# Ten query blocks' score maxima crossed over the partitions by VectorE and a line in DRAM, in an attention and mixture-of-experts kernel

## The chip, the core and the metric

The kernel runs on one core of one Trainium2 chip. The time is device microseconds of one launch; the profile is one further execution, taken by the hardware profiler. Engines are named as in the profile: PE (TensorE, with PEld for its weight loads), DVE (VectorE), ACT (ScalarE), POOL (GpSimd) and SP (SyncE), whose queue of DMA issues is shown as SPq.

## What is computed

One layer in float32, on 4096 tokens of 256 features: causal attention with one head of 256, then eight experts of which each token takes two.

```python
# x: (1, 4096, 256)
z = layernorm(x)
Q, K, V = z @ Qw, z @ Kw, z @ Vw
scores = Q @ K.T / sqrt(256) + causal_mask
x = x + softmax(scores) @ V

h = layernorm(x) @ W_in + b_in
probs = softmax(h @ W_gate + b_gate)            # 8 experts
topv, topi = top_k(probs, 2); topv /= topv.sum()
mid = relu(h @ W1[e] + b1[e])                   # for the experts taken
x = x + (sum_e topv[e] * (mid @ W2[e] + b2[e])) @ W_out + b_out
```

The softmax subtracts, from each query's scores, the largest of them. That maximum is what this change is about.

## The kernel before

**Layout.** Scores are held transposed: keys on the 128 partitions, queries along the free dimension. A query block is 256 queries (`QB`); there are sixteen, numbered 0 to 15. A chunk is 256 keys (two key tiles of 128). Block n needs chunks 0 to n. `scores(n)` makes, for each chunk, eight PE instructions into one PSUM tile `ps` (four such tiles exist, shared under the tag "mm" with the tiles `pq` and `ph`), a copy to SBUF by ACT (`s`, L564), and a running maximum over chunks by DVE (`mx`, L570). At its end DVE folds the two halves of `mx` and the diagonal chunk into `top`, 128 partitions by 256 queries (L588 to L591): on each partition, for each query, the largest of the scores that this partition holds. What is still wanted is the maximum over the partitions, and that on every partition.

**The maximum over the partitions before.** It is done in the inner function `finish` of `scores`. PE turns `top` in two 128 by 128 squares into PSUM (`pt`, L598), DVE reduces along the free dimension (`m`, L603), and PE turns `m`, broadcast, back in two more squares (`pmax`, L608). Then DVE subtracts `pmax` from every chunk of the block's scores (L612, and L618 for the diagonal chunk) and ACT takes the exponentials (L615, L621).

**The loop.** Iteration g computes `scores(g + 1)`, then `attend(g)`: for each chunk c of block g eight PE instructions (six for the diagonal one) accumulate `po` (two tiles under the tag "o", of which there are two in all, shared with the tiles `pv` of `values` and `pk` of `route`). After chunk c `attend` runs what stands in the list `between[c]`; from iteration 4 on (`CALM`) that is where `finish` of block g + 1 is put, at chunk min(g - 2, 4), with its first turn kept in program order on PE. At the end of `attend` DVE takes the reciprocal of the sums (`rinv`, L645) and adds the result to `x` (L647), which sets `po` free.

Around that, in even iterations `project` (`pq` on PE, copied to `qT` by DVE at L518) and `values` (`pv`, L526) follow for the next 512 tokens, and from iteration 6 on `send` runs at chunk 5: `ph` on PE (L362, four tiles that take all four "mm" tiles), then `lg` and `hr` on DVE (L372, L373), then two DMAs of `hr` to DRAM (`rows`, L375). In iterations 3 and 5 `send` comes ahead of `attend`. `route` (L399 to L458, with the matmuls `pk` at L423 and L428) follows the iteration of its `send`, or in iterations 3 and 5 its `attend`.

**SP's queue.** Each 512 tokens' normalised rows are turned, twice per 512 tokens (`zT` for the attention, `z1T` for the experts), by a DVE transpose of 32 by 32 squares (L329) and sixteen DMAs from SP (`move` in `turn_todo`, L334), each of 32 KB. So nearly every iteration of the attention has one set of sixteen DMAs in SP's queue. SP issues in order, and an issue that waits holds what is behind it.

**Order.** The framework's scheduler lists the instructions of each engine in an order of its own, by priority (program order) among what it takes to be ready; `tc.keep_in_program_order` pins an instruction. The order on each engine is fixed before the run.

Of the kernel before, what the change touches and what calls it, by code (L numbers as in the profile page):

```python
# [10 lines left out]
F32 = mybir.dt.float32  # L11
I32 = mybir.dt.int32
AF = mybir.ActivationFunctionType
ALU = mybir.AluOpType
AX = mybir.AxisListType
SP = mybir.EngineType.SP

P = 128
# [3 lines left out]
QB = 256  # L22
# [6 lines left out]
SQ = 32  # L29
LATE = 2  # L30
USUAL = 6
CALM = 4
# [5 lines left out]
def preln_attention_moe_kernel(  # L38
# [18 lines left out]
    nc = tc.nc  # L57
# [3 lines left out]
    NT = S // P  # L61
# [28 lines left out]
    dram = ctx.enter_context(tc.tile_pool(name="dram", bufs=1, space=bass.MemoryType.DRAM))  # L90
    attn = ctx.enter_context(tc.tile_pool(name="attn", bufs=1))
# [14 lines left out]
    slots = dram.tile([NE * R, LINE], I32, name="slots")  # L106
    bias1 = dram.tile([NE * P, NF], F32, name="bias1")
    parts = dram.tile([TOPK * S, D], F32, name="parts")


    zeros = const.tile([P, P], F32, tag="zeros", name="zeros")
# [46 lines left out]
    for b in range(1, NB):  # L158
# [13 lines left out]
        out=mask,  # L172
        in_=mask,
        compare_op=ALU.is_ge,
        fill=MASKED,
# [360 lines left out]
    KU = QB // P  # L536
    QPB = TB // QB

    def scores(g, fill=()):

        b, q = divmod(g, QPB)
        parts_of = min(max(g - 1, 1), 4)
        ss, mx = [], None
        top = attn.tile([P, QB], F32, tag="top", name=f"top{g}", bufs=2)
        for c in range(g + 1):
            ps = ps_mm(f"ps{g}_{c}")
            s = piece(f"s{g}_{c}", KU, QB)
            ss.append(s)  # L550
            for u in range(KU):
                kt = c * KU + u
                lo = u * P if c == g else 0
                for d in range(ND):
                    nc.tensor.matmul(  # L555
                        ps[:, u * QB + lo : (u + 1) * QB],
                        lhsT=zT[kt // TPB][:, kt % TPB, d, :],
                        rhs=qT[b][:, d, q * QB + lo : (q + 1) * QB],
                        start=(d == 0),
                        stop=(d == ND - 1),  # L560
                    )
            flat = s.rearrange("p u q -> p (u q)")
            if c < g:
                nc.scalar.copy(flat, ps)  # L564
                if c == 0:
                    mx = flat
                else:
                    old = mx
                    mx = attn.tile([P, TB], F32, tag="mx", name=f"mx{g}_{c}", bufs=2)
                    done = nc.vector.tensor_tensor(mx, ps, old, ALU.max)  # L570
                    for do in fill[len(fill) * (c - 1) // parts_of : len(fill) * c // parts_of]:
                        if done:
                            tc.keep_in_program_order(done)
                        done = do()
                    if fill and done:
                        tc.keep_in_program_order(done)
                continue
            for u in range(KU):
                on = slice(u * P, (u + 1) * P)
                nc.vector.tensor_tensor(  # L580
                    s[:, u, on], ps[:, u * QB + u * P : u * QB + (u + 1) * P], mask, ALU.add
                )
                if u + 1 < KU:
                    nc.scalar.copy(s[:, u, (u + 1) * P :], ps[:, u * QB + (u + 1) * P : (u + 1) * QB])
            if mx is None:
                nc.vector.tensor_copy(top, s[:, 0, :])
            else:
                nc.vector.tensor_tensor(top, mx[:, :QB], mx[:, QB:], ALU.max)  # L588
                nc.vector.tensor_tensor(top, top, s[:, 0, :], ALU.max)
            for u in range(1, KU):  # L590
                nc.vector.tensor_tensor(  # L591
                    top[:, u * P :], top[:, u * P :], s[:, u, u * P :], ALU.max
                )
        def finish(behind=False):

            pt = ps_tr(f"pt{g}")
            for u in range(KU):
                done = nc.tensor.transpose(pt[:, ts(u, P)], top[:, ts(u, P)], ident)  # L598
                if behind:
                    tc.keep_in_program_order(done)  # L600
                    behind = False
            m = attn.tile([P, KU], F32, tag="m", name=f"m{g}", bufs=2)
            nc.vector.tensor_reduce(  # L603
                m, pt[:, :QB].rearrange("p (u k) -> p u k", k=P), AX.X, ALU.max
            )
            pm = ps_tr(f"pmax{g}")
            for u in range(KU):
                nc.tensor.transpose(pm[:, ts(u, P)], m[:, u : u + 1].to_broadcast([P, P]), ident)  # L608
            for c in range(g + 1):
                s = ss[c]  # L610
                if c < g:
                    nc.vector.tensor_tensor(  # L612
                        s, s, pm[:, :QB].unsqueeze(1).to_broadcast([P, KU, QB]), ALU.subtract
                    )
                    nc.scalar.activation(s, s, AF.Exp)  # L615
                    continue
                for u in range(KU):
                    nc.vector.tensor_tensor(  # L618
                        s[:, u, u * P :], s[:, u, u * P :], pm[:, u * P : QB], ALU.subtract
                    )  # L620
                    nc.scalar.activation(s[:, u, u * P :], s[:, u, u * P :], AF.Exp)  # L621

        return ss, finish

# [413 lines left out]
    for e in range(NE):  # L1038
# [23 lines left out]
        out=slots.rearrange("(p n r) o -> p n (r o)", p=P, r=SB // LINE),  # L1062
        in_=empty.unsqueeze(1).to_broadcast([P, NE * R // P * LINE // SB, SB]),
# [5 lines left out]
        out=rows[TOPK * (S - LATE * TB) :, :].rearrange("(t p) d -> p t d", p=P),  # L1069
        in_=zero.unsqueeze(1).to_broadcast([P, TOPK * (LATE * TPB + 1), D]),  # L1070
    )

    row, finish = scores(0)
# [4 lines left out]
    fill, lg, got, hTs = [], None, {}, {}  # L1078
    for g in range(NT // KU):
        b, q = divmod(g, QPB)  # L1080

        between = {}
        nxt = None
        if g + 1 < NT // KU:

            nxt, finish = scores(g + 1, fill)
            if g < CALM:
                finish()
            else:
                between[min(g - 2, 4)] = [partial(finish, True)]  # L1090
        fill = []
        if q == 0 and b == NB - 1:

# [4 lines left out]
        if q == 0 and b > 0:  # L1098

            def send(behind=False, b=b):  # L1100
                nonlocal lg
                lg = enter(b - 1, z1T, attn, behind)

            if b - 1 >= EASY[1]:
                between[5] = [partial(send, True)]
        if q == 0 and b == NB - 1:

            def fetch_first():
                for n in range(AHEAD):
                    got[n] += fetch_weights(work[n])  # L1110

            def find():
                nonlocal seen
                seen = route(b - 1, lg, seen, attn, True)

            between[6], between[11] = [fetch_first], [find]
            weighed = AHEAD
        elif g == 0:
            turn(0, 1, ahead, zT[1])
# [210 lines left out]
```

## Time and profile before

| | |
|---|---|
| median of 3 runs | 1080.48 us (1079.9 to 1081.41) |
| profiled execution | 1071.75 us, span 1070.0 us |
| granted TensorE clock | 1.0 |
| busy in the span: PE, PEld | 1062.3 us, 882.9 us |
| DVE, ACT, POOL | 674.6 us, 332.4 us, 236.9 us |
| turns `pt` (L598) | 32 instructions, 7.1 us |
| turns `pmax` (L608) | 32 instructions, 6.1 us |
| reduction `m` (L603) | 16 instructions, 423 ns each |
| SP's DMAs for `zT` and `z1T` | 96 and 112 issues of 32 KB |

Busy time of a group counts stretches of time, so that overlapped instructions are not counted twice; the mean of one instruction is its own length. The timeline gives the start in microseconds from the start of the span, the time covered, engine, line, operation, what is written and read, and how many were merged into the line; in square brackets stands the engine's idle time before it and what ended that. The attention lies between about 20 and 565 us; iterations 4 to 13, which the change touches, between about 83 and 479 us.

### The profile page before, as it was taken

How to read it: one execution, taken by the hardware profiler on the slowest of the kernel's cores; microseconds unless marked ns; L12 is line 12 of the kernel's file. 1: busy time of each engine (PE TensorE's matmuls, PEld its weight loads, DVE VectorE, ACT ScalarE, POOL GpSimd, SP SyncE). 2: the span in 40 equal slices, each digit the busy share in tenths (PEclk: the TensorE clock that was granted, in tenths of full speed). 3: DMA queues.
4: the chain of work that ended last, by engine and by line, in shares of the span. 5: the costliest groups of instructions: out<-in, count | busy, mean ns of one | idle time of the engine just before them, and what ended most of it. 6: DMA issues, size and time to landing. Idle time of an engine off the chain costs nothing.

```text
span 1070.0 us, 15770 instructions
## 1 busy us (share of the span) xinstructions
PE 1062.3 (99%) x4973; PEld 882.9 (83%) x4973; DVE 674.6 (63%) x2114; ACT 332.4 (31%) x730; POOL 236.9 (22%) x289
## 2 busy tenths in 40 slices
PE   9999999999999999999999999999999999999998
PEld 6788888888888888888888887777778787777887
DVE  5877667564655546254665724858588786767636
ACT  2232233322432323242402221232323332323254
POOL 2104043103103000201222522232322322313110
PEclk9999999999999999999999999999999999999999
DMA  9422211121011011001655475887889896969285
GB/s 313 104 54 44 58 25 51 17 54 24 6 45 25 8 21 39 3 1 21 202 170 180 124 248 180 280 266 268 279 269 315 262 333 213 335 211 327 77 300 187
DMA packets 177995, 158.80 MB, mean 148 GB/s; under 512 B 82158, under 2 KB 157875, under 8 KB 177909
## 3 DMA queue, kind: packets, MB, share of 16 engines
q1 hardware_dynamic: 168980, 139.67, 42.4%
q0 software_dynamic: 8384, 17.58, 5.1%
q8 instruction: 40, 0.66, 0.3%
q10 hardware_dynamic: 544, 0.52, 0.1%
q14 instruction: 47, 0.38, 0.1%
HBM read 124.79 MB, written 26.38 MB: 141 GB/s over the span
## 4 chain that ended last, share of the span: by engine, by line
PE 97%; DVE 2%; POOL 0%; DMA 0%; issue 0%; SPq 0%; ACT 0%; DVEq 0%; POOLq 0%
PE po L633 21%; PE ps L555 21%; PE pm_a L921 11%; PE pe_a L988 11%; PE pe_b L988 5%; PE pm_b L921 5%; PE ph L362 3%; PE pm_c L951 3%; PE pf L1209 3%; PE pe_c L988 3%; PE pq L511 3%; PE pv L526 2%; PE pe_d L988 2%; PE pm_d L951 2%; PE pm_z L921 1%; PE pe_z L988 1%
## 5 line engine op out<-in xcount | busy, mean ns | idle before, releaser
L633 PE MATMUL po<-v,s 128*128 128x257 f32 x1056 | 237.9, 380 | 0.0
L555 PE MATMUL ps<-qT,zT 128*128 128x256 f32 x1088 | 233.3, 374 | 0.0
L555 PEld LDWEIGHTS ps<-qT,zT 128*128 128x128 f32 x1088 | 203.1, 190 | 28.0 <-issue 1.0
L633 PEld LDWEIGHTS po<-v,s 128*128 128x128 f32 x1056 | 197.2, 190 | 26.7
L564 ACT COPY s<-ps 128x512 f32<-128x512 f32 x120 | 70.2, 585 | 171.9 <-PE ps L555 132.6
L988 PE MATMUL pe_a<-w_a,mid_a 128*128 128x256 f32 x544 | 121.6, 380 | 0.0
L921 PE MATMUL pm_a<-hT_a,w_a 128*128 128x256 f32 x544 | 120.0, 379 | 0.0
L988 PEld LDWEIGHTS pe_a<-w_a,mid_a 128*128 128x128 f32 x544 | 102.6, 190 | 19.0 <-issue 5.6
L570 DVE TENSOR_TENSOR mx<-ps,mx 128x512 f32<-128x512 f32 x91 | 62.9, 691 | 83.7 <-ACT s L564 82.9
L930 ACT ACTIVATE mid_a<-pm_a,c_a 128x256 f32<-128x256 f32 x136 | 64.2, 472 | 165.1 <-PE pm_a L921 150.4
L921 PEld LDWEIGHTS pm_a<-hT_a,w_a 128*128 128x128 f32 x544 | 103.4, 190 | 14.1
L615 ACT ACTIVATE s<-s 128x512 f32<-128x512 f32 x120 | 72.2, 630 | 100.2 <-DVE s L612 100.2
L901 DVE STREAM_TRANSPOSE hT_a<-h_a 32x128 f32<-32x128 f32 x272 | 82.2, 302 | 3.8
L443 POOL DMA_INDIRECT slots<-assign,ati x64 | 62.5, 977 | 77.5 <-DVE ati L441 58.7
L612 DVE TENSOR_TENSOR s<-s,pmax 128x512 f32<-128x512 f32 x120 | 73.0, 679 | 7.3 <-PE pmax L608 7.3
L997 POOL DMA_INDIRECT parts<-y_a,slot_a x34 | 34.2, 1005 | 167.4 <-DVE y_a L996 138.0
L893 DVE STREAM_TRANSPOSE mid_c<-raw_c 32x256 f32<-32x256 f32 x128 | 55.8, 436 | 1.9
L988 PE MATMUL pe_b<-w_b,mid_b 128*128 128x256 f32 x256 | 56.8, 380 | 0.0
L921 PE MATMUL pm_b<-hT_b,w_b 128*128 128x256 f32 x256 | 56.6, 379 | 0.0
L988 PEld LDWEIGHTS pe_b<-w_b,mid_b 128*128 128x128 f32 x256 | 48.5, 190 | 9.4 <-issue 2.8
L921 PEld LDWEIGHTS pm_b<-hT_b,w_b 128*128 128x128 f32 x256 | 48.6, 190 | 6.6
L930 ACT ACTIVATE mid_b<-pm_b,c_b 128x256 f32<-128x256 f32 x64 | 30.1, 470 | 63.0 <-PE pm_b L921 63.0
(280 smaller groups left out, 1163.5 us busy)
## 6 DMA issues: line engine op xcount, KB each, us to landing
w_a<-in_L_ffn_W_dram SPq DMA_DIRECT2D x68, 512.0 KB, 6.0
w_d<-in_L_ffn_W_dram SPq DMA_DIRECT2D x48, 512.0 KB, 6.8
w_c<-in_L_ffn_W_dram SPq DMA_DIRECT2D x32, 512.0 KB, 8.1
w_b<-in_L_ffn_W_dram SPq DMA_DIRECT2D x32, 512.0 KB, 7.8
rows<-hr SPq DMA_DIRECT2D x16, 512.0 KB, 3.2
yp<-parts SPq DMA_DIRECT2D x14, 512.0 KB, 7.0
x<-in_L_attn_x_dram SPq DMA_DIRECT2D x7, 512.0 KB, 4.2
z1T<-z SPq DMA_DIRECT2D x112, 32.0 KB, 2.0
```

The lines of the kernel that those rows point to most:

```text
L443: put = nc.gpsimd.indirect_dma_start(out=slots, out_offset=bass.IndirectOffsetOnAxis(ap=ati[:, j : j + 1], axis=0), in_=assign[:, TOPK * ( ...
L555: nc.tensor.matmul(ps[:, u * QB + lo : (u + 1) * QB], lhsT=zT[kt // TPB][:, kt % TPB, d, :], rhs=qT[b][:, d, q * QB + lo : (q + 1) * QB], ...
L564: nc.scalar.copy(flat, ps)
L570: done = nc.vector.tensor_tensor(mx, ps, old, ALU.max)
L612: nc.vector.tensor_tensor(s, s, pm[:, :QB].unsqueeze(1).to_broadcast([P, KU, QB]), ALU.subtract)
L615: nc.scalar.activation(s, s, AF.Exp)
L633: nc.tensor.matmul(po[u][:, : D + 1], lhsT=ss[c][:, k, ts(u, P)], rhs=vb[kt // TPB][:, kt % TPB, :], start=(kt == 0), stop=(kt == g * KU + u),
L893: pin(do())
L901: pin(do())
L921: nc.tensor.matmul(pm[:, :SB], lhsT=w1[c][:, ts(f, P)], rhs=hT[:, c, :], start=(c == 0), stop=(c == ND - 1),)
L930: nc.scalar.activation(mid[f // 2][:, f % 2, :], pm[:, :SB], AF.Relu, bias=c1[:, f : f + 1])
L988: nc.tensor.matmul(pe[ts(j, rest), :D], lhsT=mid[f][:, ts(u, P)][:, ts(j, rest)], rhs=w2[f // (NF // 2)][:, f % (NF // 2), :], start=(f == 0),
```

## The change

For the blocks 5 to 14, whose scores are made in iterations 4 to 13 (`far`), the maximum over the partitions no longer goes through PE. At the end of `scores` the new function `spread_top` transposes `top` in place in 32 by 32 squares on DVE, reduces each square's rows (`m4`, 128 by 8), copies the four groups of 32 partitions beside each other (`c4`) and reduces over them (`m`, 32 by 8). SP writes `m` to a line of 256 numbers in DRAM (`tops`, two lines used in turn), and reads that line back, broadcast to 128 partitions, into `top`. `finish` then subtracts `top` from SBUF in place of `pmax` from PSUM. It is put two chunks later: after chunk min(g - 1, 6). The six other blocks keep the turns, now in the function `top_by_pe`.

```diff
+    tops = dram.tile([2, QB], F32, name="tops")
...
-    def scores(g, fill=()):
+    def scores(g, fill=(), far=False):
...
+        def spread_top():
+            nc.vector.transpose(top, top)
+            m4 = attn.tile([P, QB // SQ], F32, tag="m4", name=f"m4_{g}", bufs=2)
+            nc.vector.tensor_reduce(
+                m4, top.rearrange("p (b k) -> p b k", k=SQ), AX.X, ALU.max
+            )
+            c4 = attn.tile([SQ, P // SQ, QB // SQ], F32, tag="c4", name=f"c4_{g}", bufs=2)
+            for k in range(P // SQ):
+                nc.vector.tensor_copy(c4[:, k, :], m4[ts(k, SQ), :])
+            m = attn.tile([SQ, QB // SQ], F32, tag="m1", name=f"m1_{g}", bufs=2)
+            nc.vector.tensor_reduce(m, c4.rearrange("p k b -> p b k"), AX.X, ALU.max)
+            home = tops[g % 2 : g % 2 + 1, :]
+            nc.sync.dma_start(out=home.rearrange("o (b i) -> (o i) b", i=SQ), in_=m)
+            nc.sync.dma_start(out=top, in_=home.to_broadcast([P, QB]))
+
+        if far:
+            spread_top()
+
         def finish(behind=False):
-            pt = ps_tr(f"pt{g}")
-            ...
-            for u in range(KU):
-                nc.tensor.transpose(pm[:, ts(u, P)], m[:, u : u + 1].to_broadcast([P, P]), ident)
+            pm = top if far else top_by_pe(behind)
             for c in range(g + 1):
...
+        def top_by_pe(behind):
+            # the turns and the reduction as they stood in finish
+            ...
+            return pm
...
-            nxt, finish = scores(g + 1, fill)
+            far = CALM <= g < NT // KU - 2
+            nxt, finish = scores(g + 1, fill, far)
             if g < CALM:
                 finish()
             else:
-                between[min(g - 2, 4)] = [partial(finish, True)]
+                between[min(g - 1, 6) if far else 4] = [partial(finish, True)]
...
-                between[5] = [partial(send, True)]
+                between.setdefault(5, []).append(partial(send, True))
...
-            between[6], between[11] = [fetch_first], [find]
+            for c, do in ((6, fetch_first), (11, find)):
+                between.setdefault(c, []).append(do)
```

## The prediction

> **What bounds the kernel now.** I read the page's busy line and its chain first, then the chain in order of time through iterations 4 to 13, then the timeline of SP's queue, then all engines together where a wait could reach PE.
>
> ```profile
> PE 1062.3 (99%) x4973; PEld 882.9 (83%) x4973; DVE 674.6 (63%) x2114; ACT 332.4 (31%) x730; POOL 236.9 (22%) x289
> PE 97%; DVE 2%; POOL 0%; DMA 0%; issue 0%; SPq 0%; ACT 0%; DVEq 0%; POOLq 0%
> ```
>
> PE is busy for 99% of the span and is 97% of the chain that ended last, at a granted clock of 1.0. What leaves PE leaves the time, and any wait that reaches PE is added to it.
>
> ```profile
> 91.78 5.21 PE po L633 x24
> 97.21 0.87 PE po L633 x4
> 98.30 2.17 PE po L633 x10
> 100.47 3.43 PE pq L511 x8
> 103.90 3.45 PE pv L526 x16
> ```
>
> This is iteration 4 in the chain (start, length). Between the first two lines lie 0.22 us, the two turns `pt`; between the next two 0.22 us, the two turns `pmax`. Nothing else is missing: DVE's reduction between them is covered by four `po`. The turns' own rows (7.1 and 6.1 us of busy time for 32 each) count overlapped stretches; the gaps in the chain are what they cost.
>
> ```profile
> 87.76 10.40 SPq L334 DMA_DIRECT2D z1T<-z  x16
> 117.98 11.68 SPq L334 DMA_DIRECT2D zT<-z  x16
> 129.75 1.10 SPq L375 DMA_DIRECT2D rows<-hr  x2
> 144.11 10.44 SPq L334 DMA_DIRECT2D z1T<-z  x16
> ...
> 180.88 10.99 SPq L334 DMA_DIRECT2D zT<-z  x16
> 209.94 10.41 SPq L334 DMA_DIRECT2D z1T<-z  x16
> ```
>
> SP's queue in iterations 4 to 8. Each set of sixteen issues holds it for over 10 us, 0.65 us an issue, though one such DMA lands in 2.0 us (median). The sets end at 98.16, 129.66, 154.55, 191.87 and 220.35.
>
> ```profile
> 93.09 0.29 DVE L591 TENSOR_TENSOR top<-top,s 128x128 f32<-128x128 f32 x1
> 97.25 0.42 DVE L603 TENSOR_REDUCE m<-pt 128x2 f32<-128x256 f32 x1 [3.86 <-PE pt L598]
> 98.33 3.08 DVE L612 TENSOR_TENSOR s<-s,pmax 128x512 f32<-128x512 f32 x5 [0.67 <-PE pmax L608]
> ...
> 101.86 0.22 DVE L645 RECIPROCAL rinv<-po 128x1 f32<-128x1 f32 x2
> 102.22 0.69 DVE L518 COPY qT<-pq 128x512 f32<-128x512 f32 x1
> 102.83 0.86 DVE L647 SCALAR_TENSOR_TENSOR x<-po,rinv,x 128x256 f32<-128x256 f32 x2
> ...
> 103.74 3.62 PE L526 MATMUL pv<-vw,zT 128*128 128x256 f32 x16
> ```
>
> Iteration 4 on all engines. `top` is whole at 93.4, DVE idles 3.9 us, subtracts from 98.33, and only then frees `po`, whose first tile is free near 103.3; `pv` takes that tile at 103.74. The early iterations have half a microsecond to spare here, no more. Iteration 6 is as tight at another place:
>
> ```profile
> 161.67 0.41 DVE L373 TENSOR_TENSOR hr<-ph,bin 128x256 f32<-128x256 f32 x1
> ...
> 162.40 3.60 PE L511 MATMUL pq<-zT,qk 128*128 128x512 f32 x8
> ```
>
> `ph` holds all four "mm" tiles; the first comes free with `hr` at 162.08, and `pq` starts at 162.40.
>
> **What the change removes.** Four turns for each of ten blocks: 0.43 to 0.44 us of chain each, 4.35 us in all. DVE loses a reduction of 0.42 us per block.
>
> **What it adds on DVE.** A transpose of 128x256 (L893, as long in the free dimension, 436 ns), a reduction of 256 numbers a partition (L603, 423 ns), four copies of eight numbers (L416, 164 ns), a small reduction (L440, 179 ns): 1.7 us, so 1.3 us net, 13 us over ten blocks on an engine busy 674.6 of 1070. They fall into the idle time after `top` (3.9 us in iteration 4, 7.33 us in 6 to 10). I cost them at nothing; without that cover they would be 1.7 us of delay of the subtraction, counted below anyway. The subtraction reads SBUF in place of PSUM: L589, all SBUF, takes 415 ns for 128x256, L618, from PSUM, 411. No difference.
>
> **What it adds on SP.** Two DMAs per block, twenty in all, the second waiting for the first. The write is 256 numbers of 4 bytes. No such row exists; the nearest writes to DRAM are POOL's scatters into `slots`, 2.1 us to landing. From above: the bias write (L205), also in small pieces, held SP for 7.23 us with 1024 pieces, so a quarter, 1.8 us, before landing. The read brings 128 KB from a 1 KB line. Nearest: the read of `late_slot` at 610.5 and the DMA that waited for it at 612.7, 2.2 us; from above, `slot_a<-slots` amid the weights' traffic, 5.2 us. I take 2.1 + 2.2 + 0.2 for hand-overs = 4.5 us, with 3.8 and 9 as ends; these iterations' DMA share is 0.14 to 0.26, so the low side is nearer. No gain can hide in it. While the read waits, SP's queue stands 2.1 us; behind it are `rows<-hr` and later sets of moves, all wanted many microseconds later (`zT` from 180.88 is used at 235), so that costs nothing.
>
> **When the subtraction can start.** The write stands behind the sixteen moves, which are earlier in program order. So it leaves at the later of `top` + 1.7 and the end of the set:
>
> - iteration 4: 95.1 against 98.2; subtraction at 102.7, was 98.33: 4.4 later
> - 5: 122.5 against 129.7; 134.3, was 130.87: 3.4 later
> - 6: 150.1 against 154.6; 159.1, was 156.88: 2.2 later
> - 7: 188.7 against 191.9; 196.4, was 195.41: 1.0 later
> - 8 to 11: the turns themselves had been held back, now 0.5 to 2.2 earlier
> - 12 and 13: `top` is late (402.4, 464.8); 3.0 and 4.7 later
>
> **What that does to PE.** DVE runs in order, and what stands behind the subtraction is what frees PE's tiles. I keep the order of before.
>
> - Iteration 4: first `po` tile free at 103.3 + 4.4, `pv` at 107.8 for 103.74: +4.05.
> - Iteration 5: `pk` (L423) takes a `po` tile; it ran at 136.30, with the tile free near 135.65. Now 135.65 + 3.4 + 0.1 = 139.15: +2.85.
> - Iteration 6: `hr` done at 162.08 + 2.2; `pq` at 164.4 for 162.40: +2.0.
> - Iteration 7: no "o" tile is wanted until 215.96; the score tiles have four places of 1.73 us each. Nothing.
> - 12: DVE has until 421 (`pq`), subtractions and `hr` end near 419. Nothing. 13: `rinv` moves from 478.05 to 480.2, while PE works on `ps` with four places. Nothing.
>
> These three hold their own saved turns already. The other seven save 7 x 0.435 = 3.05. Sum: 4.05 + 2.85 + 2.0 - 3.05 = +5.85 us.
>
> **A rule that says otherwise.** SP's row above is 0.65 us per issue, 10.4 us per set. The Trainium skill, "DMA: Bandwidth & Descriptors", section "Issuing engines are not separate DMA queues", holds that the sequencer's time to initiate a DMA is usually small relative to the DMA itself. By that rule the write leaves as soon as `m` is there: iteration 4's subtraction starts at 99.6, 1.3 late (0.9 on PE), 5 and 6 start early, and the sum is -3.0. By the trace's row it is +5.85. The row decides; but whoever ordered DVE's instructions by such a rule would have put the subtraction first, which makes the stall.
>
> **The rivals.** *DVE's order changes* (faster). If the scheduler expects the read to land after `attend` ends, it puts `rinv` and L647 ahead of the subtraction in iterations 4 and 5, and `hr` ahead in 6. Then nothing reaches PE; the exponentials are wanted only after the next `scores`, 12 to 16 us on. Sum -4.35: 1076.1. For it: in iteration 5 DVE already runs `route` ahead of a subtraction that waits. Against: it must know of SP's 10 us; with two DMAs of about 2 us alone the subtraction looks ready at 99.6 in iteration 4, just ahead of `attend`'s end near 100, and far ahead in 5 and 6. Iteration 4 can thus go either way alone: without its stall +2.85 + 2.0 - 8 x 0.435 = +1.4: 1081.9.
>
> *The DMA chain is long* (slower still). Each microsecond over 4.5 adds one in iterations 4, 5 and 6, and from about 6 us iteration 7 begins to count: at 6 us the sum is +10, 1090.5.
>
> *The turns stay.* If the new path were not taken, the count of `pt` would stay at 32 and nothing would change; the diff gives no reason.
>
> **How the numbers follow.** The sum is against the profiled execution (1071.75, span 1070.0); the runs' median lies 8.7 above it, and I carry the difference over: 1080.48 + 5.85 = 1086.3. Chances: three stalls 0.42; iteration 4 spared 0.13; DVE's order changed 0.38; long chain 0.07. A measurement of this kernel can tell about 0.2%, 2.2 us, from no change. Faster 0.38; within 0.2% 0.10 (most of the spared case); slower 0.52. The likeliest case's own range is 1083 to 1090. The range runs from the rival's 1076.1, less a little, to 1089.5.
>
> **What would show it.** Right: twelve turns `pt` left; `tops` written right after each set of moves; DVE waiting on a DMA ahead of the subtraction with `rinv` behind it; PE idle for about 4, 3 and 2 us near 104, 140 and 166, and none after 240. Wrong: `rinv` or `hr` ahead of the subtraction in those iterations, the write ahead of the moves, or PE's gaps gone with no new ones.

## The result: 31.6 us slower

| | before | after |
|---|---|---|
| median | 1080.48 us (1079.9 to 1081.41, 5 runs) | 1112.09 us (1111.27 to 1114.96, 5 runs) |
| profiled execution | 1071.75 us, span 1070.0 | 1113.05 us, span 1111.3 |
| granted clock, mean | 1.000 | 0.991 |

The ratio is 1.0294, 95% interval 1.028 to 1.0308. The change is slower, as forecast, but by more than five times the forecast's 5.85 us, and outside its range.

The experiments ran on five chips of two kinds. On two chips, called the first kind here, the kernel before takes 1081.7 us (1079.71 to 1083.17); on three, the second kind, 1071.5 to 1071.6 us (1071.33 to 1071.81). So every kernel is set against before on its own chip, and kernels that ran on different chips are compared within one kind only. By its times the result above is of the first kind, and before's profile is like the second. On the second kind the kernel after takes 1105.1 us (1104.1 to 1105.71) against 1071.6: ratio 1.0309 (1.0292 to 1.0327), 33.5 us. Where the 10 us of before lie is told with `e0_before`.

**The profile after.** The page's busy line first:

```profile
PE 1071.4 (96%) x4933; PEld 885.0 (80%) x4933; DVE 686.0 (62%) x2174; ACT 329.6 (30%) x730; POOL 237.5 (21%) x289
```

Forty turns fewer on PE, sixty instructions more on DVE, as the diff says. But PE is busy 9 us longer with less work, at 96% of the span where it was 99%: it waits, and part of the time it runs slower. The turns that are left, from the answer on the tile `top`, and the two DMAs, from the answer on the tile `tops` (count, then shortest, median and longest issue in ns, and first and last start):

```profile
L635 PE MATMUL pt<-ident,top x12: 272/273/332, 19.5 to 562.2; 128*128 128x128 f32 x12
```

```profile
L609 SPq DMA_DIRECT2D tops<-m x10: 85/332/545, 98.5 to 502.6; - x10
L610 SPq DMA_DIRECT2D top<-tops x10: 332/337/356, 105.2 to 510.1; - x10
```

Twelve turns are left, and the DMAs are cheap to issue. SP's timeline shows when they are issued:

```profile
87.50 10.41 SPq L336 DMA_DIRECT2D z1T<-z  x16
98.46 0.09 SPq L609 DMA_DIRECT2D tops<-m  x1
105.18 0.36 SPq L610 DMA_DIRECT2D top<-tops  x1
...
136.04 0.54 SPq L609 DMA_DIRECT2D tops<-m  x1
...
144.13 0.33 SPq L610 DMA_DIRECT2D top<-tops  x1
```

The write leaves right after the sixteen moves, at the predicted time (98.2 was forecast). The read, which waits for the write to land, leaves 6.7 and 8.1 us after it, where 2.1 was forecast. SP's and DVE's waits (total, times, longest):

```profile
SPq L610 <- DMA tops<-m: 56.7, 9, 7.1
```

```profile
DVE s L620 <- DMA top<-tops: 82.9, 9, 15.1
```

Iteration 4 on all engines:

```profile
100.97 0.48 DVE L672 SCALAR_TENSOR_TENSOR x<-po,rinv,x 128x256 f32<-128x256 f32 x1
...
103.03 1.89 PE L528 MATMUL pv<-vw,zT 128*128 128x256 f32 x8
...
108.54 3.10 DVE L620 TENSOR_TENSOR s<-s,top 128x512 f32<-128x512 f32 x5 [3.39 <-DMA top<-tops]
109.32 0.63 ACT L623 ACTIVATE s<-s 128x512 f32<-128x512 f32 x1 [17.18 <-DVE s L620]
109.86 0.35 ACT L535 COPY v<-pv 128x256 f32<-128x256 f32 x1
110.11 1.67 ACT L623 ACTIVATE s<-s 128x512 f32<-128x512 f32 x3
110.26 2.08 PE L528 MATMUL pv<-vw,zT 128*128 128x256 f32 x4 [5.34 <-ACT v L535]
```

The subtraction starts at 108.54, 10.1 us after the write's issue; 4.5 of them were in the sum. The scheduler did put `rinv` and L672 ahead of it, so `po` is free and `pv` starts, as the rival "DVE's order changes" had it. The stall comes by another queue: ACT's exponentials stand ahead of its copies of `v`, they wait for the subtraction, the copies wait behind them, and after two `pv` tiles PE has no tile left. The third starts 5.3 us late and takes 2.08 us for four instructions, twice their length at full clock. PE's next longer waits, from its own timeline:

```profile
153.32 6.65 PE L557 MATMUL ps<-qT,zT 128*128 128x256 f32 x24 [3.87 <-DVE s L626]
...
186.58 5.84 PE L557 MATMUL ps<-qT,zT 128*128 128x256 f32 x18 [4.02 <-DVE qT L520]
...
229.12 8.68 PE L557 MATMUL ps<-qT,zT 128*128 128x256 f32 x40 [2.19 <-DVE mx L572]
...
264.82 5.38 PE L528 MATMUL pv<-vw,zT 128*128 128x256 f32 x16 [3.51 <-DVE x L672]
...
355.66 3.88 PE L528 MATMUL pv<-vw,zT 128*128 128x256 f32 x16 [2.73 <-DVE x L672]
...
458.85 5.57 PE L528 MATMUL pv<-vw,zT 128*128 128x256 f32 x16 [3.55 <-DVE past L420]
...
523.56 15.81 PE L557 MATMUL ps<-qT,zT 128*128 128x256 f32 x72 [2.43 <-ACT s L566]
```

These are iterations 5, 6, 7, 8, 10, 12 and 13. The releasers up to iteration 12 are DVE's subtraction itself (`s`, L626) and `qT`, `mx`, `x` and `past`, which stand behind it on DVE. In iteration 13 it is ACT's copy `s` (L566), which stands behind the exponentials. The attention ends at 602.1 us, after 564.0 in before's profile.

### The profile page after: what moved, and what is told of

It is laid out like the page before. It is cut to its first block, busy times and chain, and to the rows that moved or that the text cites. A ratio compares the mean times of both kernels' runs of the same rounds, so it can differ in the third digit from the quotient of the medians.

```text
span 1111.3 us, 15791 instructions
## 1 busy us (share of the span) xinstructions
PE 1071.4 (96%) x4933; PEld 885.0 (80%) x4933; DVE 686.0 (62%) x2174; ACT 329.6 (30%) x730; POOL 237.5 (21%) x289
## 5 line engine op out<-in xcount | busy, mean ns | idle before, releaser
L557 PE MATMUL ps<-qT,zT 128*128 128x256 f32 x1088 | 239.1, 379 | 13.0 <-DVE qT L520 4.0
L557 PEld LDWEIGHTS ps<-qT,zT 128*128 128x128 f32 x1088 | 205.7, 193 | 44.2 <-DVE qT L520 4.7
L658 PE MATMUL po<-v,s 128*128 128x257 f32 x1056 | 234.4, 380 | 0.0
L566 ACT COPY s<-ps 128x512 f32<-128x512 f32 x120 | 69.2, 585 | 159.8 <-PE ps L557 113.8
L620 DVE TENSOR_TENSOR s<-s,top 128x512 f32<-128x512 f32 x95 | 58.7, 684 | 89.0 <-DMA top<-tops 82.9
L528 PE MATMUL pv<-vw,zT 128*128 128x256 f32 x128 | 36.1, 432 | 15.1 <-DVE x L672 6.2
```

What stands on the lines that cost most here:

```text
L557: nc.tensor.matmul(ps[:, u * QB + lo : (u + 1) * QB], lhsT=zT[kt // TPB][:, kt % TPB, d, :], rhs=qT[b][:, d, q * QB + lo : (q + 1) * QB], ...
L620: nc.vector.tensor_tensor(s, s, pm[:, :QB].unsqueeze(1).to_broadcast([P, KU, QB]), ALU.subtract)
L658: nc.tensor.matmul(po[u][:, : D + 1], lhsT=ss[c][:, k, ts(u, P)], rhs=vb[kt // TPB][:, kt % TPB, :], start=(kt == 0), stop=(kt == g * KU + u),
```

## The experiments

**The landing or the added work?** `e1_no_dma` leaves both DMAs out: it subtracts each partition's own maximum, so its output is not the reference's; DVE's spread is still computed, into a tile that nobody reads.

```diff
-            nc.sync.dma_start(out=home.rearrange("o (b i) -> (o i) b", i=SQ), in_=m)
-            nc.sync.dma_start(out=top, in_=home.to_broadcast([P, QB]))
```

> The changed kernel with its twenty DMAs left out: VectorE still turns and reduces (into a scratch tile), but the subtraction takes `top` as it stands, so each partition subtracts its own largest score and the softmax is not the reference's. PE's turns are gone for the ten blocks. Theory (the loss is the wait for the line in DRAM): nothing is left to wait for, so only the saving remains: 4.4 us faster than before, between 3 and 6. Rival (the loss is VectorE's added work, or the scheduler's new order of instructions): it stays slower than before by 10 us or more, as the changed kernel is by 31.6.

Measured 1076.48 against 1081.74 us, ratio 0.9956 (0.9942 to 0.997). Nearly all the loss goes with the DMAs. That the gain is so near the expected 4.4 us is partly luck: on chips of this kind before has a stall in iteration 4 that costs 5.2 us and that this kernel has not (told below), while this kernel has a wait of 3.95 us for `mx` in iteration 5 that has nothing to do with the DMAs. Its attention ends at 565.7 us, before's at 569.2 with the stall and at 564.0 without.

`e8_unread` does the reverse: the work is done and nobody waits for it.

```diff
-            nc.sync.dma_start(out=top, in_=home.to_broadcast([P, QB]))
+            nc.sync.dma_start(out=t2, in_=home.to_broadcast([P, QB]))   # t2: read by nobody
...
-            pm = top if far else top_by_pe(behind)
+            pm = top_by_pe(behind)
...
-                between[min(g - 1, 6) if far else 4] = [partial(finish, True)]
+                between[min(g - 2, 4)] = [partial(finish, True)]
```

> The maximum comes by TensorE's turns at the place of before, as before the change; VectorE's spread and both DMAs (4-byte pieces out, the line back to 128 partitions) are also made, on SP's queue behind the moves, into a tile that nobody reads. It holds the cost of the added work without anybody waiting for its result. Theory (the loss of the kernel after is the wait for the landed line): within 4 us of before, 1079 to 1085. Rival (the 256 pieces on SP's queue hold up SP's later moves and rows, or VectorE's added 1.7 us in each block hold up its other work): 10 us or more slower, 1091 or above, and SP's moves seen to issue later.

Measured 1081.87 against 1081.73, ratio 1.0003 (0.9993 to 1.0012). DVE's added instructions and SP's twenty issues, with SP standing some 7 us in each block, cost nothing that can be measured as long as nobody waits for their result.

**Which part of the DMA way?** `e2_contig` adds one 32 by 32 transpose on DVE, so that SP writes the same 256 numbers as eight runs of 128 bytes in place of 256 pieces of 4. `e2_again` is the same kernel on a chip of the second kind. The other engines keep their order; on DVE one piece of the subtraction changes its place besides.

```diff
-            m = attn.tile([SQ, QB // SQ], F32, tag="m1", name=f"m1_{g}", bufs=2)
+            m = attn.tile([SQ, SQ], F32, tag="m1", name=f"m1_{g}", bufs=2)    # zeroed, 8 columns used
...
+            nc.vector.transpose(mt, m)
...
-            nc.sync.dma_start(out=home.rearrange("o (b i) -> (o i) b", i=SQ), in_=m)
+            nc.sync.dma_start(out=home.rearrange("o (b i) -> (o b) i", i=SQ), in_=mt[: QB // SQ, :])
```

> The changed kernel, but VectorE turns the 32x8 result once more (one 32x32 square), so that SP writes eight runs of 128 bytes to DRAM in place of 256 single numbers of 4 bytes; one fill and one small turn per block more on VectorE. In the changed kernel's profile the read is issued 6.4 to 7.4 us after the write, and the subtraction starts 3.4 to 4.3 us after the read. Theory (the small pieces make the write slow): write to read falls to 2 to 3 us, the subtraction comes 4 us earlier in every iteration, and the loss against before falls from 31.6 us to between 6 and 16 us. Rival (any write to DRAM that a read must wait for takes that long): 6.4 us or more stay and the loss stays at 28 to 34 us.

Measured 1082.04 against 1081.74, ratio 1.0006 (0.9996 to 1.0015): better than expected, in part because before has a stall of its own on this chip, which is told below.

> The contiguous write on SP's queue, POOL's order of iteration 5 as in the kernel after. If this chip has before at 1071.6: theory (4-byte pieces are nearly all of the loss, POOL's order in iteration 5 the rest), 4 to 9 us slower than before, 1075 to 1081, so that the pieces take 25 to 30 us of the kernel after's 33.5 and POOL's order 7 to 12 here. Rival (before's stall hid nothing, the contiguous kernel equals before on every chip): 1071 to 1073.

Measured 1075.95 (1075.52 to 1076.31) against 1071.53, ratio 1.004 (1.0025 to 1.0054). On a chip of this kind the kernel after loses 33.5 us and this one 4.4, so 29 us are the 4-byte pieces. SP's timeline and SP's waits in `e2_again`, iteration 4, to be set beside those of after:

```profile
98.09 0.45 SPq L614 DMA_DIRECT2D tops<-mt  x1
99.44 0.36 SPq L615 DMA_DIRECT2D top<-tops  x1
```

```profile
SPq L615 <- DMA tops<-mt: 7.4, 9, 0.9
```

The write has landed, and the read leaves, after 1.35 us; over the whole kernel SP waits 7.4 us for it in place of 56.7. The answer on `tops` gives the read:

```profile
DMA to landing us min/median/max: 2.9/2.9/3.0
```

So this chain is 1.35 + 2.9 = 4.3 us, about the 4.5 of the forecast, which had thus sized the contiguous write.

**Is it SP's queue?** Both kernels once more with the DMAs on POOL's queue, where the sixteen moves do not stand ahead: `e5_pool` with 4-byte pieces, `e6_pool_contig` contiguous.

```diff
-            nc.sync.dma_start(out=home..., in_=...)
-            nc.sync.dma_start(out=top, in_=home.to_broadcast([P, QB]))
+            nc.gpsimd.dma_start(out=home..., in_=...)
+            nc.gpsimd.dma_start(out=top, in_=home.to_broadcast([P, QB]))
```

> The kernel after with both DMAs on POOL's queue, the write still in 4-byte pieces. Nothing of the sixteen moves stands ahead of it on its queue. Theory (the pieces themselves make the write slow, 6 to 8 us from issue to the read's issue): the write takes 5 us or more here too, and the time is near the kernel after, 1100 to 1112. Rival (the pieces are slow only because they queue behind the moves' small pieces on SP's ring): the write takes about 2 us, the time is near the contiguous write on POOL's queue (1083.7), 1081 to 1087.

Measured 1117.32 (1114.3 to 1120.17) against 1071.53, ratio 1.0422 (1.0397 to 1.0448). POOL's timeline in iteration 4:

```profile
99.07 0.69 POOL L609 DMA_DIRECT2D tops<-m  x1
106.43 0.58 POOL L610 DMA_DIRECT2D top<-tops  x1 [6.68 <-issue]
```

7.4 us from write to read on a queue without the moves: the pieces are slow, not SP's queue. The whole is worse than on SP, and slower than was expected: PE waits 10.2 us for `qT` in iteration 4 and 7.3 us for `x` in 5. Two reasons are possible and neither was tried by itself: what stands behind the waiting read on POOL's queue (scatters and layer norms), and the scheduler's order, which differs from after's on DVE, ACT and PE too.

> The write to DRAM is contiguous (one more VectorE turn makes runs of 128 bytes) and both DMAs are issued from POOL's queue, not from SP's behind its sixteen moves. Against the contiguous write on SP's queue (1082.0 us) this takes away the stand behind the moves alone, 10.4 us in each block. Theory (what is left of the DMA way's cost is the stand behind the moves): subtraction some 8 us earlier from the maximum on, 3 to 6 us faster than that kernel, 1076 to 1079, near the kernel with the DMAs left out (1076.5). Rival (POOL's queue is no freer: slots' scatters and copies of POOL stand ahead, and the DMAs' issue costs POOL): no gain, 1082 or above.

Measured 1083.74 against 1081.73, ratio 1.0025 (1.0011 to 1.0039): no gain, as the rival said (`e2_contig`, on a chip of the same kind, took 1082.04). The write leaves at 98.83, behind POOL's scatters, later than SP's 98.09, so this kernel does not take the stand away; that the stand behind the moves is harmless is shown by `e15_contig_fix` below. Another order of DVE's instructions gives one stall of 4.79 us for `qT` in iteration 4.

**The later place.** `e4_late` keeps PE's turns for all blocks and takes only the later place of the subtraction: by min(g - 1, 6) in place of min(g - 2, 4) that is one chunk later in iterations 4 to 6 and two from 7 on.

```diff
-            nxt, finish = scores(g + 1, fill, far)
+            nxt, finish = scores(g + 1, fill)
```

> All maxima go over the partitions by TensorE's turns, as before the change; only the place of the subtraction's release is that of the kernel after, two chunks later (up to position 6 in place of 4). This is placement alone. Theory (the 4-byte DMA chain is the cost, the placement by itself little): subtraction some 2 us later in the first iterations, within 3 us of before either way, 1078 to 1085. Rival (the later place makes the stalls, whatever brings the maximum): 10 us or more slower, 1091 or above, with waits for ACT's v copies in iteration 4 as in the kernel after.

Measured 1091.3 against 1081.73, ratio 1.0089 (1.0069 to 1.0109): 9.6 us slower, nearly the rival's 10, though not for its reason. `v` is not what PE waits for; its timeline has one large wait, in iteration 5:

```profile
153.79 5.50 PE L557 MATMUL ps<-qT,zT 128*128 128x256 f32 x16 [6.77 <-DVE mx L572]
```

POOL's timeline tells why, here in `e2_again`, which has the same order:

```profile
134.50 0.23 POOL L263 TENSOR_SCALAR ln1rstd<-ln1mv 128x4 f32<-128x4 f32 x1 [25.45 <-DVE ati L443]
135.21 1.37 POOL L445 DMA_INDIRECT slots<-assign,ati  x1 [0.47 <-issue]
...
145.17 0.96 POOL L445 DMA_INDIRECT slots<-assign,ati  x1 [0.30 <-issue]
146.16 1.05 POOL L264 TENSOR_TENSOR ln1rstd<-ln1rstd,half 128x4 f32<-128x4 f32 x1
```

The layer norm's second instruction (L264) has slipped behind the eight scatters of `route`, 11 us. DVE's `z` waits for it, `mx` stands behind `z`, and PE waits for `mx`, here too in `e2_again`:

```profile
147.24 0.41 DVE L273 TENSOR_SCALAR z<-x,ln1mv,ln1rstd 128x256 f32<-128x256 f32 x1 [7.47 <-POOL ln1rstd L264]
147.57 0.68 DVE L572 TENSOR_TENSOR mx<-ps,mx 128x512 f32<-128x512 f32 x1
...
148.31 6.09 PE L557 MATMUL ps<-qT,zT 128*128 128x256 f32 x16 [4.94 <-DVE mx L572]
```

In before's profile the two run together, ahead of the scatters:

```profile
137.23 0.23 POOL L261 TENSOR_SCALAR ln1rstd<-ln1mv 128x4 f32<-128x4 f32 x1 [29.05 <-DVE ln1mv L255]
137.55 1.04 POOL L262 TENSOR_TENSOR ln1rstd<-ln1rstd,half 128x4 f32<-128x4 f32 x1
```

The scheduler's order on POOL had tipped by the move of something else; it is tipped in after, `e1_no_dma`, `e2_contig`, `e4_late` and `e5_pool`, not in `e3_only4`, `e6_pool_contig`, `e7_dve` and `e8_unread`.

In `e4_late` itself the order was not undone, so there the cause is read from the trace. `e14_fix` and `e15_contig_fix` undo it alone, in the kernel after and in the contiguous one: for the rows of iteration 5 `ln_rstd` is written ahead of `route`, which puts L264 after the first scatter in place of the eighth. The other engines keep their order.

```diff
+        if q == QPB - 1 and b == 2:
+            ln_rstd(1, b)
         if late or q == 0 and EASY[1] < b < NB - 1:
             seen = route(b - 1, lg, seen, attn)
...
-            ln_rstd(1, b)
+            if b != 2:
+                ln_rstd(1, b)
```

> The kernel after with one thing undone: in iteration 5 POOL runs the power for ln1rstd after one scatter of slots instead of after eight, because its two instructions are written ahead of the routing in the program; no other engine's order changes. The placement and the 4-byte DMA way stay. Theory (the later place's loss of about 9 us, seen with TensorE's turns kept, is this order on POOL): 5 to 10 us faster than the kernel after, 1102 to 1107. Rival (in the kernel after the wait for the landed line covers it, so the order costs nothing there): 1110 to 1113.

> The contiguous write on SP's queue (1082.0 us before this edit) with the same correction of POOL's order in iteration 5. Theory (its only large stall left, 4.98 us at 150 us followed by half the clock, is POOL's order): 5 to 8 us faster, 1074 to 1077, below the kernel before. Rival (the subtraction is late there anyway, behind the line from DRAM): within 2 us of 1082.

`e15_contig_fix`: 1068.36 (1068.18 to 1068.42) against 1071.53, ratio 0.997 (0.9959 to 0.9982), 3.2 us faster than before. `e2_again`, on another chip of the same kind, was 4.4 us slower than before, so POOL's order costs that kernel 7.6 us. PE's timeline shows no wait in iterations 4 to 13, and its clock stays at 1.00. Iteration 4 on all engines:

```profile
99.25 0.48 DVE L677 SCALAR_TENSOR_TENSOR x<-po,rinv,x 128x256 f32<-128x256 f32 x1
...
103.15 3.02 PE L528 MATMUL pv<-vw,zT 128*128 128x256 f32 x12
...
103.34 3.07 DVE L625 TENSOR_TENSOR s<-s,top 128x512 f32<-128x512 f32 x5
...
104.63 0.35 ACT L535 COPY v<-pv 128x256 f32<-128x256 f32 x1
```

The subtraction starts 5.0 us later than before's 98.33. As `x` has been taken from `po` ahead of it and ACT's copy of `v` comes in time, PE goes on.

`e14_fix`: 1102.94 against 1071.53, ratio 1.0293 (1.0276 to 1.031). That lies in the theory's range, but the theory is about the difference from the kernel after, which was taken on one chip of this kind:

> The kernel after once more, beside its corrected form on the same chip. Theory (POOL's order in iteration 5 costs 5 to 8 us of it): on a chip where before takes 1071.5, some 36 to 41 us slower than before, 1108 to 1112; on one where before takes 1081.7, 1112. Rival (the order costs nothing in it): 31 to 32 us slower on either chip.

> The kernel after with POOL's order of iteration 5 corrected, beside the kernel after. Theory: 5 to 8 us faster than the kernel after on this chip. Rival: the same as the kernel after within 2 us.

1105.1 and 1103.88 against 1071.6, ratios 1.0309 (1.0292 to 1.0327) and 1.0297 (1.028 to 1.0315). The medians are 1.2 us apart and the intervals overlap: in the kernel after POOL's order costs little or nothing, and the rival holds. PE's wait in iteration 5 stays without it:

```profile
152.04 6.71 PE L557 MATMUL ps<-qT,zT 128*128 128x256 f32 x24 [3.10 <-DVE mx L572]
```

Here `mx` stands behind the late subtraction anyway. Two waits for one engine overlap; the shorter shows its price only when the longer is gone.

**Where along the attention?** `e3_only4` takes the new path in iteration 4 alone, `e11_from8` in 8 to 13 alone.

```diff
-            far = CALM <= g < NT // KU - 2
+            far = g == CALM                      # e3_only4
+            far = 2 * CALM <= g < NT // KU - 2   # e11_from8
```

> The new path in iteration 4 alone; the other nine blocks keep PE's turns at the place of before. In the two profiles, scores of iteration 5 end at 118.86 before and at 126.41 after, from starts 0.3 us apart, so iteration 4 alone lost 7.8 us, of which some 2 us ran at a lower granted TensorE clock after PE had stood still for 5 us. Theory (each iteration's loss is its own wait plus the clock after it): 7.8 us slower than before, between 6.5 and 9, with a granted clock under 1 in this iteration and 1.0 behind it. Rival (the losses come from one iteration's delay falling into the next, or from a lower clock all over): under 4 us, or a clock below 1 elsewhere too.

> The new path in iteration 4 alone. If this chip has before at 1071.6: by the trace of its first run, whose attention ends 7.6 us later than in before's first profile, 6 to 9 us slower than before. By the prediction's step for iteration 4 (4.05 us less 0.44 of turns): 3.6 us slower.

On a chip of the first kind 1084.12 against 1081.74, ratio 1.0022 (1.0012 to 1.0031), 2.4 us where 7.8 were expected; before's own stall there, 5.2 us as told next, makes up most of the difference. On the second kind 1079.37 against 1071.53, ratio 1.0072 (1.0055 to 1.0089), 7.8 us. One line of PE's timeline in `e3_again` holds it:

```profile
110.99 2.07 PE L528 MATMUL pv<-vw,zT 128*128 128x256 f32 x4 [5.98 <-ACT v L535]
```

> The new path in iterations 8 to 13 alone (six of ten blocks), the write in 4-byte pieces as in the kernel after; iterations 4 to 7 keep TensorE's turns and their place. The prediction had the subtraction earlier in 8 to 11 and later without harm in 12 and 13: by it 6 times 0.44 us faster than before. Rival, from the trace of the kernel after (3.5 us of TensorE's wait in iterations 8 and 12 each, 2.7 in 10, 2.4 in 13, and stretches at half the clock after them): 12 to 16 us slower than before.

1083.12 (1081.56 to 1084.33) against 1071.6, ratio 1.0111 (1.0094 to 1.0128): 11.5 us slower, just under the rival's 12 to 16. The iterations that were to gain lose a third of the whole.

**Before's own 10 us.** `e0_before` is the kernel before with a profile on a chip of the first kind.

> The kernel before, unchanged, with a profile of its own. Its first profile (1071.75 us, span 1070.0, clock 1.000 throughout) is about 9 us shorter than the median of its timed runs, 1080.5 to 1081.7. If that profile left out a stall that most executions have, a second profile shows it: I expect a span near 1078 to 1080, with a stall of TensorE of about 3 us and a stretch under full clock, which the first has not. Every kernel profiled since has a wait of 2.8 to 3.0 us for ACT's mid_a at the experts' start, so this is where I expect most of it. If instead the profiled executions are simply shorter, the span is near 1070 again and no new stall appears. Ratio 1.000 either way.

1081.55 against 1081.73, ratio 0.9995 (0.9985 to 1.0005). The expected stall at the experts' start is there (3.0 us for ACT's `mid_a`), and a second, not expected, in iteration 4. DVE's timeline:

```profile
100.94 0.43 DVE L603 TENSOR_REDUCE m<-pt 128x2 f32<-128x256 f32 x1 [7.59 <-remote]
```

The turns it reads started at 96.8, yet nothing starts on any engine between 98.2 and 100.9. The iteration ends 5.2 us later than in before's first profile, and the difference stays 5.2 until 564. What ends the wait is not in the trace ("remote" names no instruction), so its cause stays open. `e10_dve4`, in which iteration 4 has no turns (`far = g == CALM` in `e7_dve`, below), was meant to tell whether the stall hangs on them.

> Only the maximum of iteration 4 is spread by VectorE's squares without a DMA; all other blocks keep TensorE's turns at the place of before. The second profile of the kernel before has a stretch at 98.2 to 100.9 us in which no engine starts anything, between the turns of iteration 4 and the reduction that reads them, and loses some 5 us there; kernels without turns in iteration 4 have no such stretch. Theory (the stall hangs on the turns of this block): 4 to 6 us faster than before, 1076 to 1078, most of what the kernel with all ten blocks on VectorE's squares gains (8.8). Rival (it is a gap of the run that moves elsewhere, and the 8.8 come from ten times 0.44 us and small waits): 0 to 1 us faster, 1080.5 to 1082.

1071.09 (1070.98 to 1071.15) against 1071.53 (1071.33 to 1071.81), ratio 0.9996 (0.9986 to 1.0005). It ran on a chip of the second kind, where before has no such stall, so it cannot tell that. What it shows is the worth of one block's turns where no wait reaches PE: 0.44 us, though the ratio's interval takes in 1.

The other traces from the first kind tell part of it. Two more kernels there keep PE's turns in iteration 4, `e8_unread` and `e4_late`, and in both the reduction is as late:

```profile
101.11 0.42 DVE L641 TENSOR_REDUCE m<-pt 128x2 f32<-128x256 f32 x1 [5.52 <-remote]
```

```profile
101.14 0.42 DVE L640 TENSOR_REDUCE m<-pt 128x2 f32<-128x256 f32 x1 [7.70 <-remote]
```

The five without turns there (`e1_no_dma`, `e2_contig`, `e3_only4`, `e6_pool_contig`, `e7_dve`) have no such wait. So on these chips the stall goes with the turns. Why it does, and why the second kind is free of it, stays open.

**A version that gains.** `e7_dve` needs no DMA: four 32 by 256 transposes on DVE, whose input is `m` read 32 times over, put the maxima on all partitions.

```diff
-            home = tops[g % 2 : g % 2 + 1, :]
-            nc.sync.dma_start(out=home.rearrange("o (b i) -> (o i) b", i=SQ), in_=m)
-            nc.sync.dma_start(out=top, in_=home.to_broadcast([P, QB]))
+            wide = m.unsqueeze(2).to_broadcast([SQ, QB // SQ, SQ])
+            for k in range(P // SQ):
+                nc.vector.transpose(top[ts(k, SQ), :].rearrange("p (b i) -> p b i", i=SQ), wide)
```

> The changed kernel with no DMA and the right result: the 32 maxima per square are spread by VectorE itself, four turns of 32x256 whose input is the 32x8 result broadcast along the free dimension, one turn for each group of 32 partitions. VectorE gets four turns of 0.44 us more, so the subtraction can start about 3.6 us after `top`, by now ahead of where the turns on PE stood. Theory (only the wait for DRAM lost the time): 3.5 to 4.5 us faster than before, about 1076 us. Rival (VectorE's own work, 3 us a block, delays what frees PE's tiles): no gain or a loss of up to 10 us, with VectorE busy where PE waits.

1072.96 against 1081.74, ratio 0.9914 (0.9898 to 0.9931): twice what was expected, since before's stall in iteration 4 is absent from it. On the second kind:

> The maximum spread over the partitions by VectorE's squares alone, without a DMA, in all ten blocks. On a chip where before has its stall near 97 us: 8 to 9 us faster than before, as measured. On one where it has none: only the turns' 10 times 0.44 us less what is left of waits, 3 to 4.4 us faster, 1067 to 1068.5.

1068.05 (1067.94 to 1068.23) against 1071.6, ratio 0.9967 (0.9955 to 0.998), 3.55 us faster, as expected. DVE's timeline in iteration 4:

```profile
93.31 0.45 DVE L598 STREAM_TRANSPOSE top<-top 128x256 f32<-128x256 f32 x1
...
95.39 1.78 DVE L610 STREAM_TRANSPOSE top<-m 32x256 f32<-32x256 f32 x4
97.20 3.10 DVE L622 TENSOR_TENSOR s<-s,top 128x512 f32<-128x512 f32 x5
```

From `top` to the subtraction 3.9 us, all in DVE's idle time; the subtraction starts 1.1 us earlier than in before's profile. It and `e15_contig_fix` beat both kernels, by a third of a percent.

## Why the prediction was wrong

Two steps failed: the size of the DMA chain, and the way in which its wait reaches PE. That the time is set by PE and that the wait is for the landed line was right. The sign was right by luck. With a chain of the forecast's length, the forecast's way costs nothing: `e15_contig_fix` is 3.2 us faster than before. What makes `e2_again` 4.4 us slower, near the forecast's 5.85, is POOL's order, which is not in the sum. By steps:

- **The turns' saving, 0.435 us a block**: 0.44 in `e10_dve4`; 3.2 and 3.55 us for ten in `e15_contig_fix` and `e7_again`, of which the second keeps one wait of 1.18 us in iteration 5. About right.
- **DVE's and SP's added work hidden**: `e8_unread`, 1.0003. Right; the spread takes 2.05 us (93.31 to 95.36), 1.7 was forecast.
- **The write behind SP's moves**: 98.46 in iteration 4 for a forecast of 98.2. Right. So the row was the better guide than the rule weighed against it (the Trainium skill, "DMA: Bandwidth & Descriptors", section "Issuing engines are not separate DMA queues", by which the time to initiate a DMA is usually small). But the stand alone is harmless: with it, the contiguous kernel is faster than before.
- **The DMA chain, 2.1 + 2.2 + 0.2 us with 9 as the upper end.** This step failed. The write takes 6.4 to 8.1 us to the read's issue, and from there 3.2 to 4.3 us pass to the subtraction: 10.1 to 12.4 us in all. The row taken for the write (scatters, 2.1 us) has no 4-byte pieces. The bound from above came from the bias write, a quarter of the time it held SP; but that is issue time, 0.54 us here, and the pieces take their time after the issue. The Trainium skill, "DMA: Bandwidth & Descriptors", section "Anatomy of one DMA — SWDGE (gpsimd) path", has a fixed cost of about 2 us for a DMA that POOL issues, most of it the wait for the write's receipt, and little for descriptors. From POOL, the contiguous write agrees (2.15 us to the read's issue, 98.83 to 100.98 in `e6_pool_contig`) and the 256 pieces do not (7.4 us in `e5_pool`); the measurement decides. Making the pieces longer, at the price of one small fill and turn on DVE, takes 29 of the 33.5 us away. Pieces of 128 bytes are also fewer, so the runs do not tell the length of the pieces from their number.
- **"I keep the order of before" on DVE.** This step failed too. The scheduler put `rinv` and L672 ahead of the subtraction in iterations 4 and 5 and the first `hr` ahead of it in 6, as the rival had it. In `e15_contig_fix` the subtraction starts 5.0, 4.0 and 5.7 us later than before in these iterations, more than the forecast's 4.4, 3.4 and 2.2, and PE waits for nothing. But the rival's sum of -4.35 holds only with a short chain, as `e15_contig_fix` shows with -3.2. Missed was ACT's queue, on which the exponentials, also waiting, stand ahead of the copies of `v`. Iteration 4 alone loses 7.8 us (`e3_again`); 4.05 was forecast, with its saved turns already in it (the expectation of `e3_again` takes them off twice).
- **Nothing in iterations 7 to 13, 3.05 us gained.** Wrong by the term of the chain: 11.5 us lost in 8 to 13 (`e11_from8`). The rival "the chain is long", at a chance of 0.07, had one microsecond per microsecond in iterations 4 to 6 and then 7; the waits came in eight of the ten.
- **PE's clock, taken as 1.0.** Not in the sum. In after it falls to a half at five of the eight waits shown above, those of 3.51 us and more; the last section has the numbers of `a1_after`.
- **POOL's order** in iteration 5: not foreseen. In after it hides behind the chain; in the contiguous kernel it is 7.6 us.
- **The start of the sum.** The 8.7 us by which before's runs lie above its profile were carried over whole. On such a chip 5.2 of them lie in iteration 4 (`e0_before`) and go with PE's turns there, which the kernel after has not, so they should not have been carried over whole. In the end this is a small term: the change costs 31.6 us on the first kind and 33.5 on the second.

The whole closes for after on the second kind. From the start of iteration 4's `pq` to the end of the attention, the windows' sums of `a1_after`, then of before's profile:

```profile
sum 497.90, PE 470.84 PEld 398.73 DVE 277.47 ACT 141.55 POOL 78.20; mean PE 94.17 PEld 79.75 DVE 55.49 ACT 28.31 POOL 15.64
```

```profile
sum 463.70, PE 463.58 PEld 397.87 DVE 266.27 ACT 143.10 POOL 77.76; mean PE 92.72 PEld 79.57 DVE 53.25 ACT 28.62 POOL 15.55
```

34.2 us more, of which PE is idle 26.9 (27.06 against 0.12) and busy 7.3 longer, in spite of the turns it no longer has: waits, and a slower clock with them.

## What to carry to other kernels

What a small DMA cost here was its landing, and with the same kilobyte and under 0.6 us of issue that went from 1.4 to 6.7 us with smaller pieces. So size such a DMA from a row with pieces of the same length, and lay the data out in one turn on an idle engine first. When a value arrives late, follow every engine whose queue holds a waiter, the second in the chain too (here ACT behind DVE), and price the clock that a stalled PE loses. After any such change compare each engine's order with the one before: a tipped pair on POOL, which is idle 79% of the time, cost 7.6 us, and was visible only once the larger wait was gone.

## What was not expected of the hardware

The same kilobyte takes 5.95 to 7.7 us (`a1_after`) from the write's issue to the dependent read's in 256 pieces of 4 bytes, and 1.2 to 1.6 us in eight of 128 bytes (`e2_again`).

PE's granted clock goes to exactly half during or after waits, in `a1_after` in four stretches that together are 17 us long. Three windows of it (length, PE's busy time, four more engines, then the clock, DMA share and GB/s):

```profile
106.00:110.50 4.50, 0.00 (x0) 0.00 (x0) 1.67 (x3) 0.88 (x3) 0.00 (x0) 0.80 0.15 29
110.50:112.50 2.00, 1.94 (x5) 1.58 (x6) 2.00 (x6) 2.00 (x6) 0.00 (x0) 0.50 0.00 0
...
352.00:354.00 2.00, 2.00 (x6) 1.56 (x6) 1.97 (x9) 0.37 (x1) 0.00 (x0) 0.50 0.03 8
```

A wait of 5.31 us brought 6.8 us at half speed; one of 2.43 us, at 349, brought 3.4 us; ones of 3.51 and 3.23 us, at 257 and 182, none. The Trainium skill, "TensorE: Matmul & The Clock Gate", "Part 1: The HAM clock gate", has half clock after an idle window of some 3.4 us, the window running free of the kernel. The halves agree, and the stretches are one or two times 3.4 us long. That 2.43 us were enough once and 3.51 not shows that the length of the wait alone does not tell.

And before's 10 us between chips: the trace shows where they lie (two stalls) and not why.
